# Layer 0's spectra from half the row frequencies, and its attention on two frequency columns at once

## The chip, the cores and the metric

The kernel runs on one core of a Trainium2 chip. The metric is the device time of one execution in microseconds (us). Five engines work beside each other, each through its own queue of instructions in order: PE (TensorE, matrix products into PSUM), DVE (VectorE), ACT (ScalarE), POOL (GpSimd) and SP (SyncE, which here issues the DMA transfers). Everything is computed in fp32; an fp32 matrix product appears in the profile as two records.

## The reference, cut to what matters

x is 4 x 32 x 128 x 128: 4 batches of T = 32 images of 128 x 128. Layer 0, which is the layer that the change edits, normalises x by groups of four columns, and then computes, for each batch:

```python
xn = _inorm(xa)                               # each image by its own mean and variance
k = _fno_layer(xn, Kcw, Ksw, 64, 64)          # 32 heads; spectral weights on the low
q = _fno_layer(xn, Qcw, Qsw, 64, 64)          # 32 x 17 frequencies, plus a skip weight
v = _fno_layer(xn, Vcw, Vsw, 128, 128)
scores = einsum('bntk,bnsk->bnts', q, k) / 64
av = einsum('bnts,bnsk->bntk', softmax(scores), v)
p = _fno_layer(av, Pcw, Psw, 128, 128)        # back to one image
a = _inorm(p + xa)
m = _fno_layer(_inorm(a), m0cw, m0sw, 128, 128, inner_norm=True, act=True)    # with a gelu
m = _fno_layer(m, m1cw, m1sw, 128, 128, inner_norm=True)
x = x + a + _inorm(m)
```

Here `_fno_layer` adds a scaled copy of its input to a spectral convolution (rfft2, weights on the low frequencies, irfft2). Layer 1 is an attention between the tokens and a mixture of 8 experts. It follows layer 0 and the change does not touch it.

## The kernel before

The Fourier transforms are matrix products with cosine and sine tables. An image, with its 128 columns on the partitions, is multiplied by a table of 64 row frequencies, real and imaginary (128 columns, `rows`): that is the first step, which leaves `z`. The second step multiplies by a table of the 33 column frequencies, real and imaginary. Attention is computed in frequency space: the scores of images t and s are sums over frequencies of products of their spectra with weights (`w_re`, `w_im`) of the heads. Only the low 32 of 64 row frequencies and the 17 lowest column frequencies have weights of their own; all others take part in one sum that has the same weight for all (`so`).

Layer 0 is a Python loop over four batches, written out, with this order in each batch b:

1. The value stage (from line 777): spectra of x are read from DRAM (`xd`) as broadcasts `xb` (line 834), copied to PSUM (`xw`, line 843), multiplied by the values' weights `gb` on POOL (line 852) and DVE (line 854), and multiplied with the probabilities `pr` on PE (`po`, line 791). `gb` is made once, at the start, from `gd` (lines 519 and 524).
2. The inverse transform, statistics, the first masked layer and its gelu. `spectra(0, q)` is the transform; the gelus are on ACT (line 1059), in an order fixed by `in_order`, which puts each behind the one before.
3. `spectra(1, gl)`, the transform of the gelu's output. Its first step (`first_step`, line 261; matrix products at line 266) takes 4 images at a time into a PSUM tile `pz`, which `evacuate` (line 197) copies out to `z1`, two of three times on ACT (line 201) and one of three on DVE (line 203). Its second step is at line 962, in four groups of 32 PSUM partitions in turn. Then come the energies: `sqx` on ACT (line 964), `weighed` on DVE (lines 991 and 1000), with sums over the partitions by PE (line 351).
4. `image_scales` (line 410) for the next batch: the sums `my` by PE (line 351) end it, together with the table `colg` and the scale `ysc` of each image.
5. `spectra_of_images` (line 450) for the next batch's x, in groups of 8 images. The first step goes into `pz` (line 266), ACT copies it into `z` with a negated copy of its real part (lines 270 and 271), DVE adds a `shift` to two columns (line 463). One group later the second step (`forward`, lines 280 and 281) takes two accumulating matrix products of 67 columns for each image into `px`, and DVE multiplies it by `ysc` into `xx` (line 473), sets the mean's entry (line 483), and eight DMAs (line 485) write `xd`.
6. `attention_weights` (line 534): DVE and ACT transpose the low columns into `xe` (line 545), `xm` (line 548) and a PSUM copy `xp`. PE sums all the high columns in `so` (16 products, lines 562 and 565). Then for each of the 17 low columns, products of every image with the 17 images from it onward (128 x 544 elements) are made for real and imaginary parts: `pa` on DVE (line 575), `pb` on POOL (line 577), or on DVE where the column's number is 2 modulo 3. PE weights them into `sp` (line 590) and `sp0` (line 592). At column 4 DVE spreads `so` into `sod` (line 580). `spt` (line 594, ACT) copies the sums, `sc` (lines 601 to 611, PE) turns them into scores, and the softmax follows (lines 614 to 621, `ex` on ACT at line 618), with `ph` on POOL (line 626). SP writes `ph` to DRAM as `prd` (line 638) and reads it back as `pr` (line 642).
7. In the meantime the end of the present batch: 32 scalings on ACT (line 1132), ordered behind the copy of `xp`; four additions on POOL (line 1142), ordered behind the last `pb`; the inverse transform (`back`: lines 314, 328 and 330), ordered behind the last scores, and 32 updates on DVE (line 1161). Between the two halves of the images, `skip_matrix` multiplies `ph` into `cm` (line 654) and DVE reduces it (lines 658 to 664). DMAs store the result.

For batch 0, steps 5 and 6 stand alone at the start, beside the preparation of the weights. For the last batch, 5 and 6 are absent and layer 1's first work begins.

The order in each engine's queue is made by a scheduler from the written order, the dependencies and the extra orders that `behind` adds. PSUM tiles rotate: the tags "a", "b" and "wide" have two buffers each. The products `pa`, `pb`, `sod`, `spt`, `ex`, `ph` and `u` share six SBUF buffers (tag "pr").

Of the kernel before, what the change touches and what calls it, by code (L numbers as in the profile page):

```python
# [7 lines left out]
F32 = mybir.dt.float32  # L8
# [5 lines left out]
P = 128  # L14
# [3 lines left out]
KA = 17  # L18
GI = 8
# [16 lines left out]
def _constants():  # L36
# [11 lines left out]
    cols1 = np.concatenate([cc[:, 32:33], cs, cc], 1) / NPIX  # L48
    cols2 = np.concatenate([0 * cc[:, :1], -cc, cs], 1) / NPIX
# [15 lines left out]

    group = (p[:, None] // 4 == p[None, :] // 4) / (4.0 * NPIX / C * T)
    of_group = p[:, None] // 4 == np.arange(32)[None, :]
    by_p = np.concatenate(
        [rows, inv_rows, cols1, cols2, same, block, comb.reshape(P, 96), pairs, group, of_group / 4]
# [6 lines left out]
NX = 1 + 2 * KY  # L76
NY = KY - 1
NCONST = 128 + 128 + 2 * NX + 32 + 4 + 96 + 64 + P + 32 + 3 * NY + 2 * P
# [30 lines left out]
def layer0(  # L109
# [51 lines left out]
    cols1, cols2 = columns(NX), columns(NX)  # L161
# [15 lines left out]

    w_re = const.tile([P, KA, NH], F32, name="w_re")
    w_im = const.tile([P, KA, NH], F32, name="w_im")
    qk = const.tile([NH, NH], F32, name="qk")  # L180
# [80 lines left out]
    def first_step(images, z, copy=None):  # L261

        for k in range(0, GI, 4):
            pz = ps.tile([P, 4, P], F32, name="pz", tag="a")
            for j in range(4):
                nc.tensor.matmul(pz[:, j], images[k + j], rows, start=True, stop=True)  # L266
            if copy is None:
                evacuate(z[:, k : k + 4, :P], pz)
                continue
            copy(z[:, k : k + 4, :P], pz)  # L270
            nc.scalar.activation(z[:, k : k + 4, P:], pz[:, :, :64], AF.Copy, scale=-1.0)

    def forward(z, c1, c2, take):


        n = c1.shape[1]
        for k in range(0, GI, 4):
            px = ps.tile([P, 4, n], F32, name="px", tag="b")
            for j in range(4):
                nc.tensor.matmul(px[:, j], z[:, k + j, :P], c1, start=True, stop=False)  # L280
                nc.tensor.matmul(px[:, j], z[:, k + j, 64:], c2, start=False, stop=True)
            take(k, px)
# [110 lines left out]
    def group_moments(sv, earlier=None):  # L393
# [11 lines left out]
        shift = one("shift", 2)  # L405
        for k in range(2):
            nc.vector.tensor_scalar(shift[:, k : k + 1], gm, 256.0 * k - 128.0, None, ALU.mult)
        return sv, gm, gv, shift

    def image_scales(sv, gm, gv, shift):  # L410
# [10 lines left out]
        n = 1 + 2 * KY  # L421
        colg = small.tile([P, 2, n], F32, name="colg", tag="colg")
        nc.vector.tensor_scalar(colg[:, 0], cols1[:, :n], gr, None, ALU.mult)
        nc.vector.tensor_scalar(colg[:, 1], cols2[:, :n], gr, None, ALU.mult)
# [25 lines left out]
    def spectra_of_images(b, xt, normed):  # L450
# [3 lines left out]
        n = 1 + 2 * KY  # L454
        xx = modes.tile([P, T, n], F32, name=f"xx_{b}", tag="xx")
        xd = dram.tile([T, 2, KX, KY], F32, name=f"xd_{b}")
        steps = []
        for g in (*GROUPS, None):
            if g is not None:
                z = grp.tile([P, GI, 192], F32, name="z", tag="z")  # L460
                first_step([xt[:, g + t] for t in range(GI)], z, nc.scalar.copy)
                for k in range(2):
                    nc.vector.tensor_scalar(
                        z[:, :, k * P], z[:, :, k * P], shift[:, k : k + 1], None, ALU.add
                    )
                steps.append((g, z))
                if g == 0:
                    continue
            g, z = steps.pop(0)

            def scaled(k, px):
                i = slice(g + k, g + k + 4)
                nc.vector.tensor_tensor(
                    xx[:, i], px, ysc[:, i].unsqueeze(2).to_broadcast([P, 4, n]), ALU.mult
                )

            forward(z, colg[:, 0], colg[:, 1], scaled)

            i = slice(g, g + GI)

# [1341 lines left out]
```

## Time and profile before

| what | us |
|---|---|
| three runs | 3008.99, 3011.21, 3016.02 (median 3011.21) |
| the profiled execution, whole | 3011.81 |
| its span | 3010.1 |
| layer 0, up to the first product of layer 1's attention | 923.06 |
| layer 1 | 2087 |
| mean granted TensorE clock | 0.977 of full speed |
| start of the inverse transform (`py`) in batches 0 to 3 | 154.94, 367.47, 578.43, 791.83 |

In the profile each line names the source line, the engine, the operation, the tile written and the tiles read, the shapes and the count, and behind the bar the busy time, the mean time of one instruction in ns, and how long the engine sat idle before them with the instruction that ended that idle time. In the views of the order in time each line begins with the start of a group and its length in us. A line number like 266 or 201 that lies in a helper collects the calls of several stages, so that the tile's name is needed to tell them apart (`pz<-cst,g` is the transform of the gelu's output, `pz<-cst,x` that of x). The four batches of layer 0 have nearly the same period, 211 to 213 us from one `py` to the next.

### The profile page before, as it was taken

Reading aid. Unit: us, or ns where it says so; the run is one execution under the profiler, and the core shown is the slowest. Engines: PE = TensorE matmul, PEld = TensorE weight load, DVE = VectorE, ACT = ScalarE, POOL = GpSimd, SP = SyncE. Lnnn points to the kernel's source line nnn. Section 1 sums busy time; section 2 is a strip of 40 time slices with the busy share of each in tenths; the row PEclk is TensorE's granted clock in tenths of the full one; section 3 lists DMA queues with packets and bytes.
Section 4 is the critical chain, followed back from the end, with each engine's and each line's share of the span. In section 5 each row is a group of like instructions: output and inputs, shape, how many; then the busy total and the mean of one; then the engine's idle time right before and its main releaser. Section 6 shows DMA issues by size and latency. Waiting matters only on the chain.

```text
span 3010.1 us, 52870 instructions
## 1 busy us (share of the span) xinstructions
PE 2793.9 (93%) x19530; PEld 1395.6 (46%) x19530; DVE 2227.6 (74%) x5029; ACT 2315.2 (77%) x3168; POOL 2054.8 (68%) x1825
## 2 busy tenths in 40 slices
PE   7789899989877999999999999989999999999997
PEld 5366466665643443433444434444444344444443
DVE  5786877778866677875668688766778766777877
ACT  2544544554447999989999999999999998999992
POOL 1703704606514997788887978898887889798773
PEclk9899999999988999999999999999999999999998
DMA  5501502304102101001110100111010010100000
GB/s 130 150 7 32 152 1 72 113 1 108 63 19 74 32 1 39 8 1 35 36 25 15 25 15 8 32 33 32 11 30 15 8 43 23 31 10 24 15 15 14
DMA packets 151731, 112.91 MB, mean 38 GB/s; under 512 B 36046, under 2 KB 139825, under 8 KB 150833
## 3 DMA queue, kind: packets, MB, share of 16 engines
q1 hardware_dynamic: 148209, 107.44, 13.6%
q8 instruction: 154, 2.52, 0.4%
q10 hardware_dynamic: 3264, 2.10, 0.2%
q14 instruction: 104, 0.85, 0.1%
HBM read 68.53 MB, written 20.00 MB: 29 GB/s over the span
## 4 chain that ended last, share of the span: by engine, by line
PE 60%; POOL 12%; ACT 10%; DVE 8%; issue 5%; DMA 1%; POOLq 0%; SPq 0%; DVEq 0%; ACTq 0%
PE d L1616 20%; PE po L1635 11%; PE px L1522 6%; ACT r L1666 4%; PE n L1616 4%; POOL e L1675 3%; POOL e L1674 3%; PE po L791 2%; PE pz L266 2%; POOL u L852 2%; ACT e L1682 2%; PE px L962 2%; POOL kx L1281 1%; DVE r L1671 1%; POOL x L1281 1%
## 5 line engine op out<-in xcount | busy, mean ns | idle before, releaser
L1671 DVE TENSOR_TENSOR r<-n,r 128x1024 f32<-128x1024 f32 (+1 forms) x1056 | 961.5, 952 | 478.8 <-PE n L1616 400.8
L1674 POOL TENSOR_TENSOR e<-r 128x512 f32<-128x512 f32 x528 | 673.3, 1275 | 271.4 <-DVE r L1671 270.9
L1666 ACT ACTIVATE r<-d 128x1024 f32<-128x1024 f32 (+1 forms) x1056 | 792.8, 802 | 66.8 <-PE n L1616 57.3
L1678 ACT ACTIVATE r<-r 128x1536 f32<-128x1536 f32 x528 | 783.6, 1484 | 16.8
L1675 POOL TENSOR_TENSOR e<-e,r 128x512 f32<-128x512 f32 x528 | 671.2, 1271 | 41.4
L1616 PE MATMUL d<-qe,ke 32*128 32x512 f32 (+3 forms) x2304 | 606.4, 602 | 39.7 <-ACT r L1666 36.1
L1635 PE MATMUL po<-e,kx 128*128 128x512 f32 (+3 forms) x1152 | 594.4, 605 | 17.2 <-POOL e L1687 17.2
L1616 PE MATMUL n<-qe,ke 32*128 32x512 f32 (+3 forms) x2304 | 606.2, 601 | 0.0
L1616 PE MATMUL n<-qf,kf 32*128 32x512 f32 (+3 forms) x2304 | 552.3, 554 | 0.0
L1616 PE MATMUL d<-qf,kf 32*128 32x512 f32 (+3 forms) x2304 | 551.1, 554 | 0.0
L1526 DVE SCALAR_TENSOR_TENSOR xc<-px,wgt,xc 128x128 f32<-128x128 f32 x1024 | 358.1, 350 | 42.7 <-PE px L1522 10.2
L1682 ACT ACTIVATE e<-e 128x512 f32<-128x512 f32 x528 | 325.8, 617 | 66.1 <-POOL e L1675 65.3
L1635 PEld LDWEIGHTS po<-e,kx 128*128 128x128 f32 x1152 | 175.4, 188 | 394.3 <-issue 308.1
L1616 PEld LDWEIGHTS d<-qe,ke 32*128 32x128 f32 x2304 | 176.7, 183 | 359.4 <-ACT r L1666 339.5
L1616 PEld LDWEIGHTS d<-qf,kf 32*128 32x128 f32 x2304 | 220.2, 186 | 175.5 <-issue 163.1
L1522 PE MATMUL px<-we,x2t 128*128 128x512 f32 x512 | 266.0, 605 | 7.2 <-DVE xc L1526 5.9
L852 POOL TENSOR_TENSOR u<-xb,gb 128x858 f32<-128x858 f32 (+1 forms) x112 | 221.2, 2015 | 49.5 <-PE po L791 45.9
L1616 PEld LDWEIGHTS n<-qf,kf 32*128 32x128 f32 x2304 | 228.2, 185 | 20.0 <-issue 12.6
L976 POOL TENSOR_TENSOR spec<-part,part 128x512 f32<-128x512 f32 x16 | 24.9, 1554 | 305.0 <-DVE part L973 149.5
L854 DVE TENSOR_TENSOR u<-xw,gb 128x858 f32<-128x858 f32 (+1 forms) x208 | 215.8, 1106 | 20.5 <-PE po L791 8.8
L791 PE MATMUL po<-u,pr 128*32 128x429 f32 (+1 forms) x1280 | 150.5, 534 | 37.6 <-POOL u L852 21.1
L1616 PEld LDWEIGHTS n<-qe,ke 32*128 32x128 f32 x2304 | 177.8, 183 | 9.8 <-DVE r L1671 1.3
(398 smaller groups left out, 3597.1 us busy)
## 6 DMA issues: line engine op xcount, KB each, us to landing
xb<-xd SPq DMA_DIRECT2D x128, 214.5 KB
xc<-x SPq DMA_DIRECT2D x29, 512.0 KB
x<-x SPq DMA_DIRECT2D x16, 512.0 KB
qf<-qe SPq DMA_DIRECT2D x64, 128.0 KB
out<-xc SPq DMA_DIRECT2D x15, 512.0 KB
x<-in_x SPq DMA_DIRECT2D x14, 512.0 KB
xb<-xd SPq DMA_DIRECT2D x32, 198.0 KB
gb<-gd SPq DMA_DIRECT2D x4, 1056.0 KB
```

The lines of the kernel that those rows point to most:

```text
L852: nc.gpsimd.tensor_tensor(u, xb, gk, ALU.mult)
L854: weighed_last = nc.vector.tensor_tensor(u, xw, gk, ALU.mult)
L1522: nc.tensor.matmul(px, x2t[:, k * P : (k + 1) * P], we[:, e0 : e0 + 4], start=True, stop=True)
L1526: nc.vector.scalar_tensor_tensor(xc[:, k], px[:, e], wgt[:, k, e0 + e : e0 + e + 1], xc[:, k], ALU.mult, ALU.add)
L1616: nc.tensor.matmul(o, k, q, start=turn == 0 or g > 0, stop=turn == 1 or g > 0)
L1635: nc.tensor.matmul(sums[c, h][:, q0 : q0 + c1 - c0], kx[:, jb], e[:, c0:c1], start=jb == 0, stop=is_last and q0 > 2 * P, skip_group_check= ...
L1666: nc.scalar.activation(r[:, g], d, AF.Ln, scale=1.0 / DSCALE)
L1671: nc.vector.tensor_tensor(r[:, g], part, r[:, g], ALU.mult)
L1674: nc.gpsimd.tensor_tensor(e, r[:, 1], r[:, 2], ALU.add)
L1675: nc.gpsimd.tensor_tensor(e, e, r[:, 0], ALU.add)
L1678: nc.scalar.activation(r, r, AF.Exp, scale=-1.0)
L1682: nc.scalar.activation(e, e, AF.Exp)
```

## The change

It has three parts.

First, `spectra_of_images`. The sums for the row frequency 64 - m follow from those for m by signs, since the image is real. The first step keeps 33 cosines and 33 sines for each image (66 columns of `rows`; `half_rows`). ACT copies 32 and 32 of them to `z`, DVE copies the two columns of frequency 32 into `z32`. The second step (`columns_of`) then takes two images as one weight matrix of 128 columns against a table of 68 columns, without the accumulating pair; ACT copies the result to `fold`. When half of the images are folded, `unfold` multiplies them by sign matrices (`of_cos`, `of_sin`, 64 partitions each): twice 8 products for `em`, the low rows in the layout that attention needs, and four for `std`, the full spectra. DVE multiplies these by `ysc` into `xe`, `xm` and `xx`. Frequency 32 goes its own way (`edge_row`) with two products, a transposition and a DMA of its own. The spectra are written by nine DMAs rather than eight.

Secondly, `attention_weights`. As only 32 low rows have their own weights, two columns, 2k and 2k + 1, now share the 128 partitions: 9 pairs instead of 17 columns, with 9 `pa`, 9 `pb` and 27 products on PE. The high rows of the low columns, which had been part of the 17 columns, move to `so`: ACT makes masked copies `hm` of the low columns, and `so` takes 34 products, each in the next of four groups of 32 PSUM partitions, rather than 16 in one group. `sod` has 128 partitions rather than 32. The transposing copies of `xe` and `xm` are gone. The tables of weights have 9 entries rather than 17 (`kq_raw` is 576 KB rather than 1088 KB), the constants 1517 columns rather than 1098.

Thirdly, the gelus. In the second half of the images, after the gelus of each of the last three groups, the first step of four images of the finished first half is issued, with a fourth behind the last; their four copies stand in ACT's fixed order. `spectra(1, gl, early)` takes these two groups as ready.

```diff
-    def first_step(images, z, copy=None):
+    def half_rows(images, z, last):
 
         for k in range(0, GI, 4):
-            pz = ps.tile([P, 4, P], F32, name="pz", tag="a")
+            pz = ps.tile([P, 4, 2, KY], F32, name="pz", tag="a")
             for j in range(4):
-                nc.tensor.matmul(pz[:, j], images[k + j], rows, start=True, stop=True)
-            if copy is None:
-                evacuate(z[:, k : k + 4, :P], pz)
-                continue
-            copy(z[:, k : k + 4, :P], pz)
-            nc.scalar.activation(z[:, k : k + 4, P:], pz[:, :, :64], AF.Copy, scale=-1.0)
-
-    def forward(z, c1, c2, take):
-
-
-        n = c1.shape[1]
+                nc.tensor.matmul(
+                    pz[:, j],
+                    images[k + j],
+                    rows.rearrange("p (r x) -> p r x", r=2)[:, :, :KY],
+                    start=True,
+                    stop=True,
+                )
+            nc.scalar.copy(z[:, k : k + 4], pz[:, :, :, :32])
+            nc.vector.tensor_copy(last[:, :, k : k + 4], pz[:, :, :, 32].rearrange("p t r -> p r t"))
+
+    def four_rows(images, z, k, copy):
+
+        pz = ps.tile([P, 4, P], F32, name="pz", tag="a")
+        for j in range(4):
+            nc.tensor.matmul(pz[:, j], images[k + j], rows, start=True, stop=True)
+        return copy(z[:, k : k + 4], pz)
+
+    def first_step(images, z):
+
         for k in range(0, GI, 4):
-            px = ps.tile([P, 4, n], F32, name="px", tag="b")
-            for j in range(4):
-                nc.tensor.matmul(px[:, j], z[:, k + j, :P], c1, start=True, stop=False)
-                nc.tensor.matmul(px[:, j], z[:, k + j, 64:], c2, start=False, stop=True)
-            take(k, px)
+            four_rows(images, z, k, evacuate)
...
+        def columns_of(g, z):
+
+            if g % half == 0:
+                folded[g // half] = grp.tile([P, pairs, 2 * n], F32, name="fold", tag="fold")
+            it = ps.tile([P, GI // 2, 2 * n], F32, name="it", tag="b")
+            for j in range(GI // 2):
+                nc.tensor.matmul(
+                    it[:, j], z[:, 2 * j : 2 * j + 2].rearrange("p t r x -> p (t r x)"), colg[:, : 2 * n], start=True, stop=True
+                )
+            k = g % half // 2
+            nc.scalar.copy(folded[g // half][:, k : k + GI // 2], it)
+
+        def unfold(a):
+
+            fold = folded[a]
+            t = slice(half * a, half * a + half)
+            scale = ysc[:, t].rearrange("p (k i) -> p i k", i=2)
+            em = ps.tile([P, 2, 512], F32, name="em", tag="wide")
+            em = em[:, :, : 2 * pairs * KP].rearrange("p i (m k y) -> p i m k y", m=2, y=KP)
+            for m, w in enumerate((slice(32, 96), slice(0, 64))):
+                for k, (trig, c0) in enumerate(((of_cos, n), (of_sin, 0))):
+                    for e in range(2):
+                        for i in range(2):
+                            r = slice(64 * i, 64 * i + 64)
+                            nc.tensor.matmul(
+                                em[64 * e : 64 * e + 64, i, m],
+                                trig[r, w],
+                                fold[r, :, c0 + e : c0 + e + 2 * KP : 2],
+                                start=k == 0,
+                                stop=k == 1,
+                            )
+            std = ps.tile([P, 2, 512], F32, name="std", tag="wide")
+            std = std[:, :, : pairs * n].rearrange("p i (k y) -> p i k y", y=n)
+            for i in range(2):
+                r = slice(64 * i, 64 * i + 64)
+                nc.tensor.matmul(std[:, i], of_cos[r, 96:], fold[r, :, n:], start=True, stop=False)
+            for i in range(2):
+                r = slice(64 * i, 64 * i + 64)
+                nc.tensor.matmul(std[:, i, :, :KY], of_sin[r, 96:], fold[r, :, :KY], start=False, stop=True)
+            for m, dst in enumerate((xe, xm)):
+                nc.vector.tensor_tensor(
+                    dst[:, :, t].rearrange("p y (k i) -> p i k y", i=2),
+                    em[:, :, m],
+                    scale.unsqueeze(3).to_broadcast([P, 2, pairs, KP]),
+                    ALU.mult,
+                )
...
+        waiting = []
+        for g in GROUPS:
+            z = grp.tile([P, GI, 2, 32], F32, name="z", tag="z")
+            half_rows([xt[:, g + t] for t in range(GI)], z, z32[:, :, g : g + GI])
+            nc.vector.tensor_scalar(z[:, :, 0, 0], z[:, :, 0, 0], shift, None, ALU.add)
+            if waiting:
+                columns_of(*waiting.pop())
+            if g == 3 * GI:
+                unfold(0)
+            waiting.append((g, z))
+        columns_of(*waiting.pop())
+        edges = edge_row()
+        unfold(1)
+        return xx, (xe, xm), xd, edges
...
+        xp = ps.tile([P, KP, T + half], F32, name="xp", tag="wide")
+        copied = nc.scalar.copy(xp, xe)
+        masked = 2 * KP
+        hm = modes.tile([P, T, masked], F32, name=f"hm_{b}", tag="hm")
+        nc.scalar.activation(hm[:, :, 1:], xx[:, :, 1:masked], AF.Identity, scale=high)
+        nc.scalar.activation(hm[:, :, 0], xx[:, :, 0], AF.Identity, scale=half_high)
...
+        same_time = [(xx[:, :, yy], xx[:, :, yy]) for yy in range(masked, 32)]
+        same_time += [(w32, x32), (xh, xs)]
+        same_time += [(hm[:, :, yy], xx[:, :, yy]) for yy in range(masked)]
+        for k, (wt, moved) in enumerate(same_time):
             nc.tensor.matmul(
-                so, x_y, x_y.unsqueeze(1).to_broadcast(twice), start=yy == KA, stop=False
+                so[32 * (k % 4) : 32 * (k % 4) + 32],
+                wt,
+                moved.unsqueeze(1).to_broadcast([moved.shape[0], 2, T]),
+                start=k < 4,
+                stop=k >= len(same_time) - 4,
             )
-        nc.tensor.matmul(so, xh, xs.unsqueeze(1).to_broadcast(twice), start=False, stop=True)
...
-        for yy in range(KA):
-            row = xp[:, yy // 9, yy % 9 * (T + half) :]
+        for yy in range(KP):
+            row = xp[:, yy]
...
+        early = []
         for g in range(1, 4):
             gelu(1, g)
+            h, k = divmod(4 * g - 4, GI)
+            if k == 0:
+                early.append(grp.tile([P, GI, P], F32, name="z1", tag="z"))
+            in_order(four_rows([gl[:, 8 * h + t] for t in range(GI)], early[h], k, nc.scalar.copy))
+        in_order(four_rows([gl[:, 8 + t] for t in range(GI)], early[1], 4, nc.scalar.copy))
...
-        spec, sq = spectra(1, gl)
+        spec, sq = spectra(1, gl, early)
```

## The prediction

> **What bounds the kernel now.** I read the page's engine totals first, then the work of each engine in stages of one period of layer 0, then the chain and the order in time inside the stage that the change edits.
>
> ```profile
> PE 2793.9 (93%) x19530; PEld 1395.6 (46%) x19530; DVE 2227.6 (74%) x5029; ACT 2315.2 (77%) x3168; POOL 2054.8 (68%) x1825
> ...
> 425.00:437.00 12.00, 6.92 (x48) 4.07 (x40) 10.71 (x46) 11.33 (x29) 0.00 (x0) 0.94 0.00 0
> 437.00:456.00 19.00, 18.92 (x165) 14.23 (x166) 8.91 (x46) 5.91 (x12) 1.27 (x1) 0.77 0.01 2
> 456.00:482.00 26.00, 25.21 (x218) 24.45 (x217) 19.50 (x76) 10.73 (x26) 2.31 (x2) 1.00 0.22 39
> 482.00:500.00 18.00, 17.80 (x118) 7.13 (x115) 15.34 (x24) 12.43 (x32) 13.42 (x13) 1.00 0.26 75
> 500.00:520.00 20.00, 16.83 (x164) 8.22 (x164) 14.37 (x42) 8.07 (x14) 15.10 (x8) 1.00 0.31 68
> ```
>
> Columns of the stage table: stretch, length, busy time of PE, weight load, DVE, ACT and POOL, granted clock, DMA share, GB/s. The stretch 425 to 520 is the passage from image batch 1 to batch 2; three such passages and one start are edited. Layer 1 (923 to 3010) is untouched. From 437 to 482 TensorE is busy end to end: first the spectra of the gelu output, then the spectra of x. From 482 to 500 DVE, POOL and PE share the attention products.
>
> ```profile
> L281 PE MATMUL px<-colg,z 128*128 128x67 f32 x64 | 12.3, 274 | 0.0
> L266 PE MATMUL pz<-cst,x 128*128 128x128 f32 x64 | 8.7, 283 | 0.1
> L562 PE MATMUL so<-xx 128*32 128x64 f32 x30 | 3.7, 295 | 0.5 <-DVE xx L473 0.5
> L575 DVE TENSOR_TENSOR pa<-xp,xe 128x544 f32<-128x544 f32 x17 | 11.4, 710 | 0.9 <-PE sc L601 0.9
> L1161 DVE SCALAR_TENSOR_TENSOR x<-four,c,x 128x128 f32<-128x128 f32 x32 | 8.7, 344 | 1.8 <-PE four L330 1.6
> ```
>
> These are groups by line. Each fp32 matmul leaves two records and the means overlap, so I use pitches: line 266 has 12 records in 1.42 us in the chain (466.09), 0.237 a matmul; the 64 matmuls of lines 280 and 281 take the rest of 456 to 478.4, 14.3 us, 0.223 each. The order in time (start, length; in brackets the idle time before and who ended it):
>
> ```profile
> 453.92 1.06 PE L962 MATMUL px<-z,cst 128*32 128x256 f32 x20
> 454.91 0.43 PE L351 MATMUL my<-sv,ones 128*128 128x64 f32 x2
> 455.18 2.50 PE L266 MATMUL pz<-cst,x 128*128 128x128 f32 x17
> ...
> 482.06 1.97 DVE L575 TENSOR_TENSOR pa<-xp,xe 128x544 f32<-128x544 f32 x3
> ...
> 500.02 1.01 ACT L594 COPY spt<-sp 128x1024 f32<-128x1024 f32 x1 [5.42 <-PE sp L590]
> ...
> 498.85 9.29 POOL L1142 TENSOR_TENSOR x<-x,g 128x1024 f32<-128x1024 f32 x4
> 508.11 3.10 POOL L626 TENSOR_TENSOR ph<-ex,sm 32x512 f32<-32x512 f32 x2
> ...
> 520.39 2.96 DVE L854 TENSOR_TENSOR u<-xw,gb 128x858 f32<-128x858 f32 x3
> ```
>
> So x's spectra take 455.3 to 482.1 (26.8 us, until the first product), the products 482.1 to 500.0 (17.9), and from there softmax, inverse and the 32 updates of line 1161 run to 520.4, where the value stage's DVE work starts. That stage has POOL and DVE about equally full (line 852: 28 x 2.01 us, line 854: 52 x 1.11, both near 57 us), so it ends as much earlier as both start earlier.
>
> **The change, part by part (one passage, b = 1 to 2).**
>
> *Early first steps.* Sixteen of the 32 first-step matmuls of the gelu output (line 266) and their four copies (line 201, 0.60 each) go among the gelus, where PE is busy 6.92 of 12 us. ACT there is full (11.33 of 12): three more copies stand before the table load, one replacing what evacuation already did, so the load at 437.43 moves by 2 to 3 x 0.47 to 0.59, say 1.4 us later. After it, the stage loses 16 x 0.237 = 3.8, and the waits for evacuation between (3.98 and 3.18 us of ACT idle at 447.85 and 453.15, where copy and matmul alternate). Queued behind the new ACT copies are the last gelus and their statistics (line 1067). Ends: 0 if the delayed gelus eat it, 7.4 if all matmuls and the first-half copies go. I take -5: the last PE work before x's, line 351's `my`, at about 450.
>
> *x's first step.* Still 32 matmuls, 66 columns wide instead of 128. The row nearest by form, line 280 (67 columns), has 0.223: 7.1 us instead of 7.5. The negative copies (line 271, 0.39 x 8 of ACT) go; eight small DVE copies of the frequency-32 column come, each behind the ACT copy of the same tile. The nearest row is line 463 (128x8), 0.28, 16 of which become 4. DVE count is thus down by 4, but the new copies free the PSUM tile (two buffers), so they now pace PE.
>
> *Second step.* 64 x 0.223 = 14.3 us become 16 x 0.223 = 3.6 us (two images' rows fill the 128 weight columns). Added per half of the images: 16 matmuls with 64 rows and 72 columns and 4 with 272; by line 962's pitch in rotating column groups (20 records in 1.06, 0.106) and by 0.223 the sixteen lie between 1.7 and 3.6, taken 1.8 (the groups rotate); the four at up to line 791's 0.45 (429 wide, 4 records in 0.91), 1.8. Twice 3.6 = 7.2, and the edge row 1. Sum of PE: 7.1 + 3.6 + 7.2 + 1 = 18.9, against 21.8 of matmuls before.
>
> The first half's unfolding stands before the last group's second step, so its evacuation is covered; the second half's stands at the end. Behind its last matmul DVE does two 144-element products (0.28 to 0.44, between lines 463 and 473), and the first attention product can start; the 544-element xe transposes (line 545, 0.67), the single-row copies of line 483 and the xm copy (line 548, 1.18 on ACT) are gone. Before, from xx (478.44) to the first product it was 3.6 us. I allow 2.4, with the ACT copy of 432 elements inside. That gives 18.9 + 0.4 fill + 2.4 = 21.7; against it DVE queues the weighed-energy work (lines 991 and 1000, four times 1.22 us at 459.7 to 464.8) ahead of z32 copies, for which I add 1. So the front is 22.5 to 23 instead of 26.8: -4. Lower end: no gain if DVE paces all eight tiles; best: -6.5.
>
> *Attention products.* 34 of 544 elements become 18: DVE 22 x 0.65 = 14.3 becomes 12 x 0.65 = 7.8; POOL 12 x 1.13 becomes 6; the matmuls of line 590 fall from 34 to 18. PE: 9 columns at (17.4 - 2 - 1)/17 = 0.85 = 7.6, plus the two `sc` of line 601 (2.0) and `so`. `so` rises from 16 to 34 matmuls. In one column group 30 records took 3.68 (0.245 each matmul); rotating over four groups, line 314 has 48 in 1.62 (502.62; 0.07), so 34 cost between 2.3 and 8.3 us; I take 2.4, for the order rotates. The `sod` spread (128 rows, same 1024 elements) costs DVE the same 1.20. New on ACT: masked copies of 544 and 32 elements, about 1.0 (line 548: 1.18); they precede `so`'s last 18, and `sod` waits for them. DVE: 7.8 + 1.2 = 9.0; PE: 2.4 + 7.6 + 2 + 1 = 13. I take the stage at 14 from the first product to `spt` (17.9 before): -4. It is no halving, since `sc` and `so` stay. ACT's 32 scales (12.43 us, line 1132) start with the products and would end at about the same time; the order puts 26 of them ahead of `spt`: 10.1 us, which fits in 14.
>
> *Downstream.* `spt` at 486.7 to 487.5 instead of 500.0. POOL's four adds (9.29) then run 485 to 494.4 and `ph` to 497.5, where it was 511.2; DVE needs `cm` from `ph` after the first 16 updates, at about 498, which fits. The 32 updates, the probabilities' transfers and `u` all shift by the same -13.
>
> Passage: -5 - 4 - 4 = -13; three passages: -39.
>
> *Start (batch 0).* No early first steps; the front starts after `my` at 23.2.
>
> ```profile
> 55.71 5.03 SPq L524 DMA_DIRECT2D gb<-gd  x2
> 60.78 21.62 SPq L834 DMA_DIRECT2D xb<-xd  x8
> 82.73 6.20 SPq L638 DMA_DIRECT2D prd<-ph  x4
> ...
> 78.30 3.08 POOL L626 TENSOR_TENSOR ph<-ex,sm 32x512 f32<-32x512 f32 x2 [7.56 <-DVE sm L621]
> 84.04 1.99 POOL L852 TENSOR_TENSOR u<-xb,gb 128x858 f32<-128x858 f32 x1 [2.66 <-PE cm L654]
> ```
>
> On SP's queue the eight `xb` loads hold `prd` until 82.7, although `ph` is ready from 81.4; the first `po` is at 94.0. In the changed order `prd` and the first `pr` stand before `xb`. Spectra and products are done about 4 + 4 + 4 earlier (products alone 18.6 us here), `ph` at some 66, but the `gb` broadcast (4.2 MB at about 120 GB/s from 36.8) still fills the queues until some 72. Then `prd`, `pr`, two `xb`, `xw`, `u`: 81 to 83 for the first `po`. Ends: 0 (transfers alone bound) and -13. I take -11.
>
> *Last batch.* Only the early first steps: -4 (-2 to -5).
>
> Sum: -39 - 11 - 4 = -54. The profiled execution's own time is 3011.81 (span 3010.1 and 1.7 around it), the median of the runs 3011.21; from either, 2957 to 2958. I say 2958.
>
> [...]
>
> **Rivals.**
>
> 1. *DVE paces x's front, and the kernel gets slower* (6%). Each first-step tile is freed by a DVE copy that stands in a queue with 1.22 us operations and waits for `ms` sums (1.31 and 0.79 us idle at 466.1 and 468.1). Those places speak for it; against it, DVE is busy 19.5 of 26 us and loses 5. Eight tiles at 3.0 plus the tail of 18 would be 42 instead of 26.8: +15 a passage, less the 9 of the other parts, 3 x 6 = +18. The start, where the same copies queue behind the weights' DVE work, gains nothing then, the last batch 4: about 3026. It decides from a front of 39 us (3 x (39 - 26.8 - 9) - 4 = 6).
>
> 2. *The start gains nothing, DMA bounds it* (15%). `gb` moves as many bytes as before, and DVE makes its source `g` in the same queue. For it: 0.54 DMA share in 53 to 72. Then 2958 + 11 = 2969.
>
> 3. *Attention doesn't shrink* (17%). If the `so` matmuls run at 0.245 after the masked copies, 34 x 0.245 = 8.3, 6 more than taken, or if POOL's adds and `ph` bind, each passage gains 7: 2958 + 18 = 2976. Against: the rotation.
>
> 4. *More goes than taken* (20%). Front -6.5, early steps -7, products -6, start -13: 3 x 19.5 + 13 + 5 = 76, 2935. The idle time of ACT at 447.85 and 453.15 speaks for it; table load and `sc` against.
>
> **How the numbers follow.** My forecast (2946 to 2966) has 40%, rivals 20, 17, 15 and 6%; 2% for no change, if a cover that I've not seen holds the end of all passages. Leaving out rival 1 and half of the outer parts of 3 and 4 gives 2934 to 2984. Within 0.2% (6 us) counts as the same, about what a measurement here can tell. Faster 0.92, same 0.02, slower 0.06.
>
> **What would show it.** Right: first `pa` of passage 2 some 22 to 23 us after `my`, `spt` 14 after that, py's 211.5 us period down to 198, layer 1's first `d` near 869. Wrong: PE idle before the narrower first step with a DVE copy as releaser (rival 1); `po` still at 94 (2); PE's `sod` or `sc` late, with the masked copies as cause (3). Layer 1 longer than 2087 us would void the sum, for I carry it unchanged.

## The result and the profile after

The changed kernel is slower: 3044.62 us in the median of four runs against 3010.57 for the kernel before, a ratio of 1.011 (95% interval 1.0093 to 1.0128). The forecast was 2958. Its profiled execution took 3043.61 (span 3041.9). Layer 1 is unchanged: its first product starts 33 us later (956.0 against 923.1) and the end comes 32 us later.

The gain that was forecast is there, and it is eaten behind it. The stage table of the passage from batch 1 to 2, with the same columns as before:

```profile
461.00:474.00 13.00, 10.24 (x69) 6.16 (x68) 11.20 (x50) 12.98 (x33) 0.00 (x0) 1.00 0.00 1
474.00:484.00 10.00, 10.00 (x117) 7.82 (x116) 6.70 (x29) 4.15 (x9) 1.27 (x1) 1.00 0.01 2
484.00:509.00 25.00, 22.74 (x187) 20.09 (x186) 17.05 (x73) 7.73 (x24) 1.68 (x2) 0.73 0.02 3
509.00:521.50 12.50, 11.38 (x130) 5.45 (x134) 9.88 (x18) 10.85 (x29) 8.01 (x7) 1.00 0.17 20
521.50:547.40 25.90, 16.67 (x160) 7.91 (x160) 14.74 (x44) 10.23 (x19) 12.45 (x7) 0.90 0.26 54
547.40:560.00 12.60, 4.94 (x32) 1.62 (x36) 6.48 (x8) 2.60 (x5) 5.15 (x3) 0.53 0.67 183
```

The spectra of the gelu's output take 10 us after the gelus where they took 18 to 19, the front 25 where it took 26.8, the products 12.5 where they took 17.9. But the stage after the products has grown from 20 to 26 us, and behind it TensorE is busy 4.94 of 12.6 us, at a granted clock of 0.53. The order in time of the changed kernel says who is late:

```profile
508.91 0.72 DVE L663 TENSOR_TENSOR pa<-xp,xe 128x544 f32<-128x544 f32 x1 [0.47 <-ACT xp L633]
...
521.50 1.01 ACT L682 COPY spt<-sp 128x1024 f32<-128x1024 f32 x1 [1.65 <-PE sp L678]
...
528.95 3.08 POOL L714 TENSOR_TENSOR ph<-ex,sm 32x512 f32<-32x512 f32 x2
544.35 2.00 POOL L937 TENSOR_TENSOR u<-xb,gb 128x858 f32<-128x858 f32 x1 [12.32 <-DMA xb<-xd]
...
543.13 0.52 ACT L928 COPY xw<-xb 128x429 f32<-128x429 f32 x1 [5.87 <-DMA xb<-xd]
543.58 0.58 ACT L356 COPY v<-y 128x512 f32<-128x512 f32 x1
...
546.33 1.13 DVE L1255 SCALAR_TENSOR_TENSOR x<-four,c,x 128x128 f32<-128x128 f32 x4 [5.75 <-PE four L358]
```

POOL's `ph` is done at 532.0. POOL, and ACT with its copy `xw`, then wait 12.3 and 5.9 us for the loads `xb` of the spectra. ACT's wait holds the copy `v` that is queued behind it, so the inverse transform and the last updates (now line 1255) are late as well: 546.3. SP's queue in the same passage, before (its transfers `xd` begin at 467.4) and after:

```profile
467.38 5.63 SPq L485 DMA_DIRECT2D xd<-xx  x4
473.18 0.62 SPq L834 DMA_DIRECT2D xb<-xd  x1
475.53 1.27 SPq L485 DMA_DIRECT2D xd<-xx  x2
476.89 0.61 SPq L834 DMA_DIRECT2D xb<-xd  x1
479.10 1.26 SPq L485 DMA_DIRECT2D xd<-xx  x2
480.53 5.16 SPq L834 DMA_DIRECT2D xb<-xd  x6
509.64 2.98 SPq L638 DMA_DIRECT2D prd<-ph  x4
```

```profile
505.70 7.75 SPq L549 DMA_DIRECT2D xd<-xx  x4
513.55 8.65 SPq L568 DMA_DIRECT2D xd<-s  x1
522.30 9.20 SPq L549 DMA_DIRECT2D xd<-xx  x4
531.60 12.79 SPq L919 DMA_DIRECT2D xb<-xd  x8
544.48 1.68 SPq L726 DMA_DIRECT2D prd<-ph  x2
```

The second number is the time that the queue spent on them, waits included. Nine writes of the spectra hold the queue from 505.7 to 531.6, the first `xb` stands until 539.6, and `prd` is issued at 544.5, 12.5 us after `ph` is done. The page of the changed kernel has the same in its groups for the whole span. The first line is that of the kernel before, where POOL waited hardly at all for `xb`:

```profile
L852 POOL TENSOR_TENSOR u<-xb,gb 128x858 f32<-128x858 f32 (+1 forms) x112 | 221.2, 2015 | 49.5 <-PE po L791 45.9
L937 POOL TENSOR_TENSOR u<-xb,gb 128x858 f32<-128x858 f32 (+1 forms) x112 | 224.1, 2046 | 133.2 <-DMA xb<-xd 95.9
L928 ACT COPY xw<-xb 128x429 f32<-128x429 f32 (+1 forms) x160 | 86.8, 545 | 140.7 <-DMA xb<-xd 102.8
```

Where the 31.8 us of the span come from, by the first `py` of each batch: the start +33.7 (188.6 against 154.9), the three passages +0.9, +1.5 and +2.6, the last batch and layer 1 together -6.8.

What is peculiar to these writes is their shape. The changed kernel leaves out row 32, so it writes rows 0 to 31 and rows 33 to 63: 32 and 31 partitions. The two kinds differ in the trace's landings (a landing is a report of arrival in the trace, which I read as one for each DMA engine with a part of the transfer; the time in the table is that of the last one):

| transfer | engines that report a landing | from issue to landing |
|---|---|---|
| before, 64 rows x 8 images, issued 467.38 | 16 | 3.1 us |
| after, 31 rows x 16 images, issued 505.70, 512.97, 522.88, 530.77 | 1 each | 10.6, 12.2, 10.6, 11.3 us |

Each of these four has right behind it an issue that stands for long: 6.0, 8.7, 7.5 and 7.9 us (issued at 506.40, 513.55, 523.27 and 531.60). Two of them are writes of 32 rows and one is the row of frequency 32 with its 8 KB, all with their data ready; the last is the first `xb`. Each of the four ends 2.5 to 3.9 us ahead of the landing of the 31 rows before it. While one of 31 rows is under way the core moves little:

```profile
507.00:512.00 5.00, 3.57 (x74) 2.48 (x67) 3.92 (x12) 3.66 (x10) 2.22 (x2) 1.00 0.11 14
514.00:522.00 8.00, 7.92 (x61) 2.60 (x53) 5.92 (x9) 6.35 (x17) 6.70 (x5) 1.00 0.11 11
524.00:531.00 7.00, 5.61 (x74) 3.24 (x74) 4.59 (x13) 3.90 (x8) 6.92 (x5) 1.00 0.10 8
```

The last two numbers of each line are the busy share of the 16 DMA engines, 0.10 to 0.11, and 8 to 14 GB/s. The landings tell of 1 engine for 31 rows, and in the runs below of 11 for 33, 15 for 15 and 16 for 32.

### The profile page after: what moved, and what is told of

It is laid out like the page before. It is cut to its first block, busy times and chain, and to the rows that moved or that the text cites. A ratio compares the mean times of both kernels' runs of the same rounds, so it can differ in the third digit from the quotient of the medians.

```text
span 3041.9 us, 52547 instructions
## 1 busy us (share of the span) xinstructions
PE 2744.7 (90%) x19442; PEld 1363.3 (45%) x19442; DVE 2198.8 (72%) x4966; ACT 2310.8 (76%) x3165; POOL 2034.0 (67%) x1801
## 4 chain that ended last, share of the span: by engine, by line
PE 56%; POOL 14%; ACT 10%; DVE 9%; issue 6%; DMA 3%; SPq 2%; POOLq 0%; DVEq 0%; ACTq 0%
PE d L1710 19%; PE po L1729 11%; PE px L1616 6%; ACT r L1760 5%; PE n L1710 3%; POOL e L1769 3%; POOL e L1768 3%; POOL u L937 3%; PE po L876 2%; ACT e L1776 2%; DMA prd<-ph 2%; DVE r L1765 2%; POOL kx L1375 2%; POOL x L1375 1%; PE pz L304 1%
## 5 line engine op out<-in xcount | busy, mean ns | idle before, releaser
L1760 ACT ACTIVATE r<-d 128x1024 f32<-128x1024 f32 (+1 forms) x1056 | 793.3, 803 | 62.0 <-PE n L1710 55.7
L928 ACT COPY xw<-xb 128x429 f32<-128x429 f32 (+1 forms) x160 | 86.8, 545 | 140.7 <-DMA xb<-xd 102.8
```

The source lines that it names most:

```text
L1760: nc.scalar.activation(r[:, g], d, AF.Ln, scale=1.0 / DSCALE)
```

## The experiments

**The shape of the writes.** The second transfer of each pair takes 32 rows, and the row of frequency 32 is written behind them, since they now overwrite it.

```diff
-                for x0, x1 in ((0, 32), (33, KX)):
+                for x0, x1 in ((0, 32), (32, KX)):
...
         unfold(1)
+        nc.sync.dma_start(out=xd[:, :, 32], in_=s32.rearrange("t (r y) -> t r y", r=2)[:, :, :KY])
```

> The changed kernel, with the second transfer of each half and part taking rows 32 to 63 (32 partitions) instead of rows 33 to 63 (31), and the row of frequency 32 written after them. Theory A: a transfer with 31 partitions is carried by one DMA engine (496 pieces of 132 bytes at about 61 a us, 8 us each, four in a row for a batch), one with 32 by all of them, and SP's queue stands behind it. Then the eight transfers land within some 3 us of their issue, the first xb comes about 5 us after the last of them and not 30, prd is issued when ph is ready, and the three passages take 13.5 us less each (from the traces: py to the end of the updates at line 1161 139.5, counted without the wait for xb, against 153.0), the last batch 5.6 less, the start 0 to 11 less: 2954 to 2965. Rival B: the transfers are slow because they are more and smaller, or hold 16 images, or wait for the frequency-32 row: then xb is as late as now and the time is 3035 to 3050. Rival C: the new first step, paced by DVE, costs what was lost: also above 3030.

Measured: 2968.22, a ratio of 0.9854 to before (0.9838 to 0.9871), 76 us below the changed kernel. SP's queue in the same passage:

```profile
463.83 7.42 SPq L549 DMA_DIRECT2D xd<-xx  x8
471.41 2.57 SPq L919 DMA_DIRECT2D xb<-xd  x3
478.03 0.60 SPq L583 DMA_DIRECT2D xd<-s  x1
478.68 3.07 SPq L919 DMA_DIRECT2D xb<-xd  x5
488.78 2.95 SPq L726 DMA_DIRECT2D prd<-ph  x4
```

Eight writes take 7.4 us, 3 of them a gap for the second half's data, and no issue behind one stands for more than 1 us. They land 3.8 to 7.6 us after their issue, which is longer than the 3 that theory A expected. `prd` is issued while `ph` runs (its second half ends at 490.3). The passages take 198.6, 197.8 and 197.9 us where they took 212.5, 211.0 and 213.4 before the change: -13.9, -13.2, -15.5. Rivals B and C fall. The edit also moves the write of the frequency-32 row to a later place in the queue. That is not what frees it: in the cut into 16 and 15 rows, below, this row keeps its place, and all thirteen writes take 8.9 us of the queue. The time is 3 us above A's range because the start does not gain but loses 6.6 (161.5).

**The shape alone, in the kernel before.** Each of its eight writes of 64 rows is cut in two, of 33 and 31 rows, and in a control of 32 and 32.

```diff
-                nc.sync.dma_start(
-                    out=xd[i, part].rearrange("t x y -> x t y"),
-                    in_=xx[64 * part : 64 * part + 64, i, 1 + KY :],
-                )
+                for x0, x1 in ((0, 33), (33, KX)):    # control: ((0, 32), (32, KX))
+                    nc.sync.dma_start(
+                        out=xd[i, part, x0:x1].rearrange("t x y -> x t y"),
+                        in_=xx[64 * part + x0 : 64 * part + x1, i, 1 + KY :],
+                    )
```

> The kernel before, with nothing changed but the writing of the spectra: each of the eight transfers of a batch (64 partitions, 8 images) is cut in two, of 33 and of 31 partitions. Theory A: both numbers lie beside a multiple of 16, each transfer of 33 or 31 rows goes through one DMA engine (264 and 248 pieces, about 4 us each), sixteen a batch, some 65 us of a queue in order: xb comes 30 us or more later in every batch, and the time rises by 60 to 200 us, 3070 to 3210. If only 31 suffers: eight of 4 us, 32 a batch, against some 15 us of slack before the first xb is needed: +10 to +25 a batch, 3050 to 3110. Rival B (number and size of the transfers): no more than the control with 32 and 32 partitions.

> The control to the cut into 33 and 31 partitions: the kernel before, each of the eight transfers cut in two of 32 partitions. Theory A: 16 transfers of 256 pieces, all spread; 8 more issues of 0.6 us on SP's queue, beside other work: 3005 to 3020. Rival B: as slow as the cut into 33 and 31.

Measured: 3039.38 with 33 and 31 (1.0084, 1.0069 to 1.0099), 3022.66 for the control (1.0029, 1.0018 to 1.0041). The first is below both sizes that were expected, the control 3 us above its range; the shape costs 17 us more than the number. The direction holds, the size does not. That 33 rows would suffer like 31, because they too lie beside a multiple of 16, is wrong: the transfers of 33 rows report 11 landings each, only those of 31 report one. The queue of the first explains the size:

```profile
495.05 29.93 SPq L486 DMA_DIRECT2D xd<-xx  x16
525.08 9.04 SPq L835 DMA_DIRECT2D xb<-xd  x8
537.30 2.97 SPq L639 DMA_DIRECT2D prd<-ph  x4
```

The writes hold the queue for 30 us here too (before: 13.0 from the first write to the end of the last). But in the kernel before, `ph` is not done until 538.9, so the queue is free in time: the passages take 212.9, 211.2 and 213.7 us, the same as before, and all the loss (27 us) lies at the start (first `py` at 182.0). In the changed kernel 26 us of writes cost the gain because there `ph` is done 26 us after the first write (505.7 to 532.0), not 44. In the control the passages are unchanged as well, and the start takes 9.4 us more, so eight more writes in the crowded start are not free.

**The third part alone, in the kernel before.**

```diff
+        early = []
         for g in range(1, 4):
             gelu(1, g)
+            h, k = divmod(4 * g - 4, GI)
+            if k == 0:
+                early.append(grp.tile([P, GI, P], F32, name="z1", tag="z"))
+            in_order(four_rows([gl[:, 8 * h + t] for t in range(GI)], early[h], k, nc.scalar.copy))
+        in_order(four_rows([gl[:, 8 + t] for t in range(GI)], early[1], 4, nc.scalar.copy))
```

> The kernel before with the third part of the change alone: the first step of the gelu output's first 16 images among the gelus. From the trace of the changed kernel, py to the end of my took 82.1 instead of 87.8 us in the passage from batch 1 to 2, and the last batch 5.6 less; so -5.7 x 3 - 5.6 = -23: 2985 to 2993. Rival: the earlier start is taken up by a later wait (POOL's additions and ph, or xb): -5.6 to -12, 2999 to 3006.

Measured: 2986.99 (0.9912, 0.9897 to 0.9926). The passages lose 6.3, 4.3 and 7.8 us, the last batch and layer 1 together 4.6; nothing takes it back later. So this part alone is worth 26 us, more than half of the 45 that the whole change is worth with 32 rows.

The trace shows something that the forecast didn't have. Before the change the granted clock was 0.50 for 10.2 us of the very stage that gets shorter, in each passage (435.6 to 445.8 in the one to batch 2, while the gelu's output is transformed). With the early first steps this is gone from two of the passages and 3.4 us are left in the third. How much of the gain is the clock's, no run separates.

**Another shape without 31.** To leave the row of frequency 32 where it was, the 31 rows are cut into 16 and 15.

```diff
-                for x0, x1 in ((0, 32), (33, KX)):
+                for x0, x1 in ((0, 32), (33, 49), (49, KX)):
```

> The changed kernel with each transfer of 31 partitions cut in two, of 16 and of 15, and nothing else moved. Theory A (a transfer rides on as many engines as the largest divisor of its rows, at most 16: 31 gives 1, 33 gave 11, 32 gives 16): 15 rows ride on 15 engines, all transfers land within 3 us, the passages are as with 32 rows (about 198 us from one py to the next), and the start loses the 8.5 us for which the frequency-32 row waited on SP's queue there (59.8 to 68.3): 2958 to 2968. Rival: only multiples of 16 are spread: each transfer of 15 rows has 240 pieces on one engine, 4 us, four a batch: 2975 to 3000.

Measured: 2992.39 (0.9943, 0.9928 to 0.9957). The time lies in the rival's range, but not for its reason. The transfers of 15 rows report 15 landings each, as A says, and arrive 3.1 to 4.3 us after their issue; yet the passages take 204.3 to 208.6 us. The queue differs:

```profile
479.61 3.05 SPq L549 DMA_DIRECT2D xd<-xx  x6
498.85 2.95 SPq L726 DMA_DIRECT2D prd<-ph  x4
503.70 0.38 SPq L730 DMA_DIRECT2D pr<-prd  x1
504.12 1.25 SPq L919 DMA_DIRECT2D xb<-xd  x2
```

With 13 writes instead of nine the scheduler put the loads `xb` behind `prd` and the first `pr`. SP issues nothing from 482.7 to 498.9, while the spectra have landed by 486.5. That led to a test of the order alone, on the kernel with 32 rows:

```diff
                     broadcast = nc.sync.dma_start(
...
+                    if b and x0 == 0 and i == 0:
+                        behind(broadcast, weights[3])
```

> The kernel with 32 rows a transfer, and one order added: in the passages the first loads xb stand on SP's queue behind the last read of pr, as they did with the cut into 16 and 15 rows (504.1 there, behind prd at 498.9), where they had been ahead of prd (471.4) with 32 rows. The cut into 16 and 15 came out 24 us slower than 32 rows, 6 to 7 a passage, with all its transfers landed in time. Theory F: the order of xb and prd on the queue is what it cost: 2968 + 3 x 6.5, 2983 to 2993. Rival G: the five more transfers a batch, or 15 rows, cost it: 2964 to 2972.

Measured: 2997.63 (0.9947, 0.9931 to 0.9964), 29 us above the kernel with 32 rows and even more than theory F expected. The passages take 209.0, 206.5 and 207.5 us. Rival G falls for this run, which has neither more transfers nor 15 rows: the order of two kinds of transfer on SP's queue is worth about 10 us a passage. Again it goes through ACT's queue: the last updates end 15.9 us behind `ph` instead of 9.6. For the cut into 16 and 15 rows the same cause is argued and not shown, since it loses in another place: there the last updates end 9.8 to 11.0 us behind `ph`, and the value stage, from the first `po` to `py`, takes 62.7 to 65.4 us instead of 59.2.

**The clock in the front.** The front of the kernel with 32 rows takes 25.0 us from `my` to the first product, some 2.3 more than forecast. Its stages:

```profile
442.00:449.50 7.50, 6.61 (x54) 6.15 (x54) 6.72 (x20) 3.61 (x10) 1.26 (x1) 1.00 0.01 2
449.50:463.20 13.70, 12.83 (x85) 11.42 (x84) 7.81 (x42) 3.02 (x10) 0.00 (x0) 0.50 0.00 0
```

The granted clock is 0.50 for 13.7 us, behind 7.5 us in which TensorE counts as busy for 6.6. Before the change the front of no passage had that, and with the third part alone there is hardly any of it (0.7 us in one passage). What it costs shows in the chain of the front, where the same 16 records (eight products of the first step) stand twice in the changed kernel, at a clock of 1.00 and then of 0.50; the third line has the wider ones before the change, at 1.00:

```profile
484.09 1.92 PE pz L290 x16
496.24 3.41 PE pz L290 x16
```

```profile
455.34 1.97 PE pz L266 x16
```

At the full clock 66 columns take as long as 128, nearly, which is what the prediction had taken; at half the clock they take 1.8 times as long. Two edits on the cut into 16 and 15 rows: the first step 128 columns wide again (more work), and the small copies on ACT.

```diff
-            pz = ps.tile([P, 4, 2, KY], F32, name="pz", tag="a")
+            pz = ps.tile([P, 4, 2, KX], F32, name="pz", tag="a")
             for j in range(4):
-                nc.tensor.matmul(pz[:, j], images[k + j], rows.rearrange(...)[:, :, :KY], start=True, stop=True)
+                nc.tensor.matmul(pz[:, j], images[k + j], rows, start=True, stop=True)
```

> As the cut into 16 and 15 rows, and the first step of x again 128 columns wide (the 66 that are used are taken from it): more work for TensorE, fewer columns used. With 32 rows the granted clock was 0.5 for 13.7 us of each passage's front (449.5 to 463.2 in the passage to batch 2) and for 27.3 us at the start, before the change 10.2 there and none in the fronts. [...]

```diff
-            nc.vector.tensor_copy(last[:, :, k : k + 4], pz[:, :, :, 32].rearrange("p t r -> p r t"))
+            nc.scalar.copy(last[:, :, k : k + 4], pz[:, :, :, 32].rearrange("p t r -> p r t"))
```

> As the cut into 16 and 15 rows, and the eight small copies of the frequency-32 columns on ACT instead of DVE. Rival E (DVE's queue paces the front and, by the waits, lowers the clock): TensorE's waits for these copies (0.2, 0.6 and 0.9 us seen in one passage) go and with them the half clock: 10 to 20 less. Theory D (the clock follows the width of the products): the waits alone, 0 to 5 less.

Measured: 2975.18 (0.9884, 0.9869 to 0.9899) and 2983.97 (0.9912, 0.9897 to 0.9927), 17 and 8 us less than the cut alone. In the wide one the half clock in the fronts shrinks from 13.7 to 23.9 us to 3.4 to 10.2, and the start from 27.3 to 6.8; the first `py` comes 11.3 us earlier. Twice the columns make the front shorter: 22.2 to 22.3 us each, against 25.1 to 26.3 with 16 and 15 rows and nothing else. But the second edit shortens the half clock in and just behind the fronts as well, to between 6.8 and 10.2 us a passage, and the fronts to 21.4 to 21.8; it leaves the first `py` where it was (163.7 against 163.5), with 34.1 us of half clock at the start. So both edits count: D's answer is right for the start, and in the fronts each of the two helps. What sets the granted clock stays open.

**The start, and the best of both.**

```diff
-    front = spectra_of_images(0, loaded, normed)
     value_weights()
+    front = spectra_of_images(0, loaded, normed)
```

> As the cut into 16 and 15 rows, and the values' weights prepared ahead of x's spectra at the start, so that gd is written near 33 us as before the change and not at 41 and 45. If the broadcast gb bounds the start (4.2 MB behind gd, then prd, pr and xb), the first po comes 5 to 8 us earlier than with the cut alone, once; all passages the same: 5 to 8 less. If the half clock of TensorE bounds it, 0, or 1 to 3 more for the later spectra.

Measured: 2987.25 (0.9924, 0.9907 to 0.9940), 5 us less than the cut alone; the first `py` comes 9.3 us earlier (154.2), part of it given back in the first passage (208.8 against 206.6) and behind the last `py` (2212.5 against 2208.3).

> 32 rows a transfer, and the first step 128 columns wide. Theory D (width keeps the clock): beside the cut into 16 and 15 rows the wide step took 11 us off the start and 3 off a passage, with half clock in the fronts down from 13.7 to 24 us to 3.4. Here 11 and 3 to 6 a passage from 2968: 2938 to 2949. If the gain there came from the late xb's slack alone: 2955 to 2960.

> As the wide step with 32 rows, and the values' weights ahead of the spectra at the start. Alone that took 5 us off, all of it before the first py but for some of the passages being longer. If broadcast and frequency-32 row on SP's queue still bound the start: 4 to 9 less than the wide step with 32 rows. If the front is the bound again: 0 to 2 more.

> All of these, and the frequency-32 copies on ACT. Alone they took 4 us off each passage (202.2 against 206.5 in the mean) by both less waiting and less half clock. With the clock already full, only the waits: 1 to 3 a passage, 3 to 9 less than without. If DVE still paces the front with the width restored: 12 less.

Measured: the wide step on 32 rows 2950.52 (0.9793, 0.9778 to 0.9807), with the weights first 2952.61 (0.9800, 0.9785 to 0.9815), with the copies on ACT too 2945.07 (0.9774, 0.9760 to 0.9789). The first of them came 1.5 us above its range; the weights first bring nothing here, since with the wide step `gd` is written at 32.9 and 34.7 already, and the first `py` comes 6.0 us later; the copies on ACT bring 7.5, within their range. The last is 68 us faster than the kernel before, and 100 faster than the changed one. The front with 32 rows and the wide step, in one stage from `my` to the first product, and its first-step products, against the narrow ones:

```profile
428.70:449.40 20.70, 17.52 (x184) 15.30 (x185) 16.90 (x72) 7.51 (x24) 1.58 (x2) 0.96 0.07 11
...
L290 PE MATMUL pz<-cst,x 128*128 128x128 f32 x64 | 8.5, 283 | 0.8 <-DVE z L292 0.6
L489 PE MATMUL it<-colg,z 128*128 128x68 f32 x32 | 4.4, 276 | 1.1 <-DVE z L568 1.1
```

```profile
442.00:467.20 25.20, 22.90 (x188) 20.14 (x187) 16.95 (x72) 7.76 (x24) 1.58 (x2) 0.73 0.07 11
...
L290 PE MATMUL pz<-cst,x 128*128 128x66 f32 x64 | 10.3, 322 | 0.9 <-DVE z L298 0.7
L495 PE MATMUL it<-colg,z 128*128 128x68 f32 x32 | 6.5, 362 | 0.9 <-DVE z L574 0.9
```

A record of the wide products takes 283 ns in the mean, one of the narrow ones 322; the second step, whose work is the same, 276 against 362. The clock is 0.96 against 0.73.

## Why the prediction was wrong

The sign was wrong by one term that the sum did not have: of the 87 us between the forecast and the measured time, the run with 32 rows takes 76 away. By its steps, in the passage from batch 1 to 2:

| step | forecast | changed kernel | with 32 rows |
|---|---|---|---|
| early first steps, `py` to `my` (87.9 before) | -5 | 82.1: -5.8 | 82.1: -5.8 |
| front, `my` to first product (26.7) | -4 | 24.8: -1.9 | 25.0: -1.7 |
| products to `spt` (18.0) | -4 | 12.6: -5.4 | 12.6: -5.4 |
| `spt` to last update (20.4) | 0 | 26.0: +5.5 | 20.1: -0.3 |
| last update to first `po` (-1.2) | 0 | 7.6: +8.8 | -1.2: 0 |
| `po` to `py` (59.2) | 0 | 59.4: +0.2 | 59.2: 0 |
| sum (211.0) | -13 | 212.4: +1.5 | 197.8: -13.2 |

**The step that failed** is "Downstream": "the 32 updates, the probabilities' transfers and `u` all shift by the same -13". It took the spectra's transfers as carried along, and the part-by-part list has no price for the nine writes that take the place of eight. Their count was known and their shape was not looked at: 31 rows, one DMA engine, four times 10 to 12 us in a row, with SP's queue behind them. The run with 32 rows gives all of the 14.6 us back (212.4 to 197.8), and the pair in the kernel before shows the shape costing time with nothing else changed.

**The start** (-11 forecast, +33.7 measured) failed by the same term, which is larger there because the spectra's writes stand ahead of three of the four `gb` loads on the queue (issued 81.8 to 91.1, before 41.2 to 60.7), and `prd` waits 28.7 us behind them to land. Without 31 rows it is still +6.6, so the -11 was wrong in more than that. `ph` is done at 74.9 there and not at some 66 (81.4 before), since the front takes 30.1 us where it took 29.2: its clock is 0.50 for 27.3 us, and I had priced it at the full clock. Then `prd` needs 18.1 us to land behind the last two `gb` loads, which are issued at 69.0 and 69.6 (before at 55.7 and 60.1). These are late because `gd` is written at 40.7 and 45.3 instead of 32.8 and 36.4, and because the row of frequency 32 stands on the queue from 59.8 to 68.3, until the writes that it overwrites have landed. No run separates what each of these is worth. The wide step brings the first `py` to 152.2 on the cut and, with 32 rows, to 149.3, 5.7 us earlier than before. There `ph` is done 16.7 us earlier than before (64.7), and the first `po` starts only 5.2 earlier (88.8): what is left of the start is bound by the transfers, as rival 2 held.

**The other terms held, one of them in part by luck.** The early first steps: -5 forecast, -5.8 measured; but the sum had them from the products and the waits for copies, and not from the 10.2 us of half clock that went with them. Behind the last `py`, -4 forecast: up to layer 1's first product the third part alone brought -3.4 and the changed kernel -5.6, and layer 1 itself was 1.1 us shorter in both. The 18 products (a stage of 14 forecast, 12.6 measured), POOL's additions and `ph` (10.5 us behind `spt`'s start; 11.2 before) and ACT's 26 scales ahead of `spt`, which fit, came as forecast. The unfolding of one half of the images, with its products of other tile sizes, took 3.3 us even at half the clock (501.36 to 504.62), where 3.6 were forecast.

The front's term was mis-sized, -4 for -1.9. The price of a product, 0.22 us, held at the full clock and was 0.43 at half of it. Rival 1's copies have a part in this, smaller than it said: TensorE's waits for them are only 0.7 us in sum, but with the copies on ACT the fronts of the cut fell from 25.1 to 26.3 us to 21.4 to 21.8, together with their half clock.

**The rivals.** None of the four names the DMA of the spectra. Rival 2 came nearest in place (the start, and the queue) but held that transfers would only keep the gain from showing. Rival 1 had the right sign, by another mechanism: its front of 42 us was 24.4 to 25.1 in the changed kernel's passages. Rival 3 falls, as the products' stage took 12.6 us. Of the signs that were to show an error, "`po` still at 94" at the start did: it was at 128.3.

## What to carry to other kernels

Of a transfer, look at the number of rows that is left when a row is cut out, not only at its bytes: here 31 rows took 10.6 to 12.2 us to land, on one engine, where 32 took 3.8 to 7.6 with several in the air, and the issue behind them stood for 6.0 to 8.7 us, which held all later transfers of the queue. A gain upstream shortens the time that a queue has for its slow work: 30 us of writes cost the kernel before nothing in its passages, and 26 us cost the faster kernel all it had won. And a matrix product cut to the columns that are needed is not always cheaper: eight products of 66 columns took 1.92 us against 1.97 of 128 at the full clock, and 3.41 at the granted clock of 0.50 that came with them.

## What the runs showed of the hardware

- A write of 31 rows reported one landing, one of 33 rows 11, of 15 rows 15, of 32 rows 16. While one of 31 rows was under way, the whole core moved 8 to 14 GB/s.
- An issue behind such a write stood for 6.0 to 8.65 us on SP's queue, the longest though it was of 8 KB, and ended 2.5 to 3.9 us ahead of the write's landing; why it stood is not shown. Long issues are not peculiar to this shape: at the start of the kernel before, an `xb` stands for 8.9 us (67.87 to 76.78) while the broadcasts `gb` are under way.
- The granted clock fell to 0.50 for 13.7 us behind a stretch of 7.5 us in which TensorE was busy 88% by the profile, and in the 8 us before it TensorE was idle for at most 0.56 us at a time. Widening the products from 66 to 128 columns removed most of it: on the cut into 16 and 15 rows 13.7 to 23.9 us in the fronts became 3.4 to 10.2, and 27.3 at the start 6.8. In the traces of the kernels before and after, the stretches at 0.50 last 3.4, 6.8, 10.2, 13.7, 17.1, 23.9, 37.5 or 61.4 us in layer 0.
